# A graph network's edge search: the second half of each list one list later, and the first layer's weights prepared behind the first list

## The chip, the cores and the metric

One Trainium2 chip, one of its cores. The metric is device time in microseconds of one execution; a kernel's time is the median of several executions.

## The reference, cut to what matters

The inputs are node features `x` (4096 x 512, float) and an adjacency `adj` (4096 x 4096 of zeros and ones, from a model in which the low nodes have many neighbours and the high ones few). Two attention layers over the graph follow each other, each with a residual and a layer norm:

```python
x = _layernorm(x + _L0_gnn_ref(x, adj, L0_gnn_W, L0_gnn_a), axis=-1)
x = _layernorm(x + _L1_gnn_ref(x, adj, L1_gnn_W1, L1_gnn_a1, L1_gnn_Wo, L1_gnn_ao, ...), axis=-1)
```

Each attention is of this form (here the first, 8 heads of 64):

```python
h = jnp.einsum('nf,kfp->knp', node_matrix, W)
f1 = jnp.einsum('knp,kp->kn', h, a_src)
f2 = jnp.einsum('knp,kp->kn', h, a_dst)
e = jax.nn.leaky_relu(f2[:, :, None] + f1[:, None, :], negative_slope=ALPHA)
e = jnp.where(adjacency_matrix[None, :, :] > 0, e, NEG_INF)
att = jax.nn.softmax(e, axis=-1)
out = jnp.einsum('knm,kmp->knp', att, h)
```

The second layer has an 8-head attention, a one-head attention of width 512 and two dense layers (512 to 1024 to 512).

## The kernel before, in words

The kernel treats the adjacency as sparse. It has two parts, one after the other. First `find_edges` turns the dense adjacency into lists of neighbours (which column, for which row); then three attention passes (`heads_layer` twice, and a last one with the dense layers) gather rows of a table of projected features by these lists, weigh and add them. A dense path (`dense_path`) stands behind a branch that is taken only if a list overflows.

**Lists.** The 4096 rows are 32 tiles of 128 rows. Tile 0, whose rows have many neighbours, is cut by columns into four lists (0 to 256, 1024, 2304 and 4096); every other tile is one list, 35 lists in all. This text counts them 0 to 34: lists 0 to 3 are tile 0, list v above that is tile v - 3.

**First half of a list: the search.** ACT turns the loaded adjacency `raw` into signs `sg` (L848, one call for a whole tile, 128 x 4096). PE builds `key`, 1024 columns at a time, by two matmuls for each 512 columns (L877: the signs; L878: a place number for each column), into two PSUM buffers. DVE finds the eight largest keys of each segment of columns (`cand`, L884; in tile 0 three times with a `match_replace`, L887, between), and then, from the candidates, the k largest in order: `lst`, k/8 rounds of L899 and L901, each dependent on the one before. `over` (L896) is taken ahead of the first round. ACT makes column numbers `qs` and a count `balance` from `lst` (L906, L909); POOL makes `degs` and `counts` (L911 to L928).

**Second half of a list: the places.** PE sums the counts over the rows before (`prs`, L931), ACT makes each row's first and last place and two rows of signs `sides` (L932 to L943), POOL adds them to `s1` (L944) and prepares `rhs` and `rest` (L952 to L955). PE then multiplies these out into `pl` (L960, the "own" matmul with `own_b`, then pairs of L967 and L969), in one piece for most lists, in three or four pieces for lists 0 to 3; `pl` has one PSUM buffer. ACT copies `nl` and, for tile 0, `kk` out of it (L971, L984). DVE picks the column (`sel`: L986 one instruction for each group of 128 edges in tile 0, L977, L980 and L981 in the other lists), and POOL writes `idx` (L992 to L994).

**Beside it.** At the end of each tile's last list the loop calls `beside(t)`: it loads 128 rows of `x`, turns them (`pt`, L683, and `xt`, L686), projects them with layer 0's weights (`ph`, L697, eight matmuls a tile) and writes table rows (`hrow`, L710 and L711). For t = 8 and t = 16 it also calls `load_projection` for the next two weights. `load_projection` loads `sw` (L654 or L659) and `sab` (L663), POOL multiplies them (`sprod`, L667) and DVE reduces (`sw_t`, L672 or L677). After the loop `project_mean` projects the mean of all rows and writes one last table row.

**What sets the order.** This stage has no hand-written order. A scheduler takes the instructions in the order in which the program text traces them, as their priority, follows a model of when each can start, and writes one fixed queue for every engine. DMAs of this stage are issued on SP. The attention passes behind it do have an order written by hand. The first gather (L1084, POOL) belongs to tile 31, the last list, and needs that list's `idx`, the table with its last row, and a gather buffer cleared by ACT (L1297).

Of the kernel before, what the change touches and what calls it, by code (L numbers as in the profile page):

```python
# [10 lines left out]
F32 = mybir.dt.float32  # L11
BF16 = mybir.dt.bfloat16
# [3 lines left out]
AF = mybir.ActivationFunctionType  # L16
OP = mybir.AluOpType
AX = mybir.AxisListType
# [3 lines left out]
P = 128  # L22
N = 4096
# [20 lines left out]
FAR = -1e30  # L44
# [514 lines left out]
def sparse_path(  # L559
# [23 lines left out]
    nc = tc.nc  # L583
# [6 lines left out]
    most = max(p.blocks for p in pts)  # L590
    longest = max(p.n for p in pts)
    kmax = max(p.k for p in pts)
# [8 lines left out]
    ident_b = const.tile([P, P], BF16, name="s_identb")  # L601
# [10 lines left out]
    half = const.tile([P, 2], F32, name="half")  # L612
# [10 lines left out]
    s1 = const.tile([P, blocks_ * P], BF16, name="s1")  # L623
# [14 lines left out]
    st0 = Stage2("t0", 8, 64, dest_first=False)  # L638
# [212 lines left out]
    def find_edges(big, sb, ps, pk, constants, sg, beside):  # L851
# [8 lines left out]
        starts = big.tile([P, nv], F32, name="starts")  # L860
        ends = big.tile([P, nv], F32, name="ends")
        degsum = big.tile([P, 1], F32, name="degsum")

        for v, p in enumerate(pts):
            t, k, c0, nch = p.t, p.k, p.first, p.n
            if t > 0:
# [28 lines left out]
            last = cand.rearrange("p (s e) -> p s e", e=r8)[:, skip:, r8 - 1]  # L895
# [9 lines left out]
            qs = sb.tile([P, kmax + 1], F32, name="qs")[:, : k + 1]  # L905
# [4 lines left out]
            deg = degs[:, v : v + 1]  # L910
# [16 lines left out]
            else:  # L927
                nc.gpsimd.tensor_copy(counts[:, v : v + 1], deg)  # L928
            deg = counts[:, v : v + 1]
            prs = ps.tile([P, 1], F32, name="prs", tag="small")  # L930
            nc.tensor.matmul(prs, before, deg, start=True, stop=True)  # L931
            nc.scalar.activation(qs[:, k:], prs, AF.Identity, bias=ends_at[:, v : v + 1], scale=-1.0)  # L932

            lim = sb.tile([P, 1], F32, name="lim")
            nc.gpsimd.tensor_sub(lim, deg, mids[:, v : v + 1])
            first = starts[:, v : v + 1]
            nc.scalar.activation(first, prs, AF.Identity, bias=mids[:, v : v + 1], scale=-1.0)
            nc.scalar.activation(ends[:, v : v + 1], prs, AF.Identity, bias=lim)
            wide = p.blocks * P
            here = s1[:, p.at * P : p.at * P + wide]  # L940
            sides = sb.tile([P, 2, most * P], BF16, name="sides")[:, :, :wide]
            nc.scalar.activation(sides[:, 0], iota_e[:, :wide], AF.Sign, bias=first)
            nc.scalar.activation(sides[:, 1], iota_e[:, :wide], AF.Sign, bias=ends[:, v : v + 1], scale=-1.0)  # L943
            nc.gpsimd.tensor_add(here, sides[:, 0], sides[:, 1])  # L944


            rhs = sb.tile([P, 2 * (kmax + 2)], BF16, name="rhs")[:, : 2 * (k + 2)].rearrange("p (h w) -> p h w", h=2)
            rest = sb.tile([P, 2 * (kmax + 1)], BF16, name="rest")[:, : 2 * (k + 1)].rearrange("p (h w) -> p h w", h=2)
            q2 = sb.tile([P, 2 * (kmax + 1)], F32, name="q2")[:, : 2 * (k + 1)].rearrange("p (h w) -> p h w", h=2)
            shape = [P, 2, k + 1]  # L950
            for h in range(2):
                nc.scalar.activation(rhs[:, h, : k + 1], qs, AF.Copy, scale=half[:, h : h + 1])  # L952
            nc.gpsimd.tensor_mul(q2, qs[:, None, :].to_broadcast(shape), half[:, :, None].to_broadcast(shape))
            nc.gpsimd.tensor_sub(rest, q2, rhs[:, :, : k + 1])
            nc.gpsimd.tensor_copy(rhs[:, :, k + 1], row1)  # L955
            per = 512 // (k + 2)
            for lo in range(0, nch, per):
                m = min(per, nch - lo)
                pl = ps.tile([P, m, k + 2], F32, name="pl")
                nc.tensor.matmul(  # L960
                    pl, ident_b, own_b[:, None, kmax - k :].to_broadcast([P, m, k + 2]), start=True, stop=False
                )
                last = None
                for block, groups, chunks in blocks_in(p, lo, m):
                    for of, w in ((rhs, k + 2), (rest, k + 1)):
                        if last:
                            nc.tensor.matmul(*last, start=False, stop=False)  # L967
                        last = pl[:, chunks, :w], s1[:, ts(p.at + block, P)], of[:, groups, :w]
                nc.tensor.matmul(*last, start=False, stop=True)  # L969
                cs = slice(c0 + lo, c0 + lo + m)  # L970
                nc.scalar.copy(nl[:, cs], pl[:, :, k + 1])  # L971
                nc.gpsimd.tensor_scalar(hole[:, cs, 0], nl[:, cs], -0.5, FAR, op0=OP.is_lt, op1=OP.mult)
                src = sb.tile([P, longest], F32, name="src")[:, :m]
                sel = sb.tile([P, 512], F32, name="sel")[:, : m * k].rearrange("p (m k) -> p m k", k=k)
                if k < 100:
                    shape = [P, m, k]
                    nc.vector.tensor_tensor(  # L977
                        sel, iota_k[:, lo : lo + m, :k], pl[:, :, k : k + 1].to_broadcast(shape), op=OP.is_equal
                    )
                    nc.vector.tensor_tensor(sel, sel, pl[:, :, :k], op=OP.mult)  # L980
                    nc.vector.tensor_reduce(src, sel, AX.X, OP.add)  # L981
                else:
                    kk = sb.tile([P, longest], F32, name="kk")[:, :m]
                    nc.scalar.copy(kk, pl[:, :, k])  # L984
                    for c in range(m):
                        nc.vector.scalar_tensor_tensor(  # L986
                            sel[:, c], iota_k[:, lo + c, :k], kk[:, c : c + 1], pl[:, c, :k],
                            op0=OP.is_equal, op1=OP.mult, accum_out=src[:, c : c + 1],
                        )

                past = sb.tile([P, longest], F32, name="past")[:, :m]
                nc.gpsimd.tensor_scalar(past, nl[:, cs], -0.5, 2.0 * N, op0=OP.is_lt, op1=OP.mult)  # L992
                nc.gpsimd.tensor_add(past, past, src)
                nc.gpsimd.tensor_copy(idx[:, cs], past)  # L994
            if p.last:
                beside(t)


        nc.vector.tensor_tensor(over[:, 1], degs, by_parts("room_k", lambda p: p.k - 0.5), op=OP.is_gt)
        groups = by_parts("room_n", lambda p: p.chunks[0] * P)  # L1000
# [369 lines left out]
    with ExitStack() as pools:  # L1370
        big = pools.enter_context(tc.tile_pool(name="eb", bufs=1))
        sb = pools.enter_context(tc.tile_pool(name="es", bufs=2))
        sg0 = signs_of(sb, 0, 8)
        constants = edge_constants(big)
        load_projection(big, st0, w0, a0)
        ps = pools.enter_context(tc.tile_pool(name="ep", bufs=1, space=PSUM))
        pp = pools.enter_context(tc.tile_pool(name="eq", bufs=2, space=PSUM))
        pk = pools.enter_context(tc.tile_pool(name="ek", bufs=2, space=PSUM))

        def beside(t):  # L1380
            xr = sb.tile([P, F], F32, name="xr")
# [16 lines left out]
    sb = ctx.enter_context(tc.tile_pool(name="ls", bufs=2, reuse_waits="tile"))  # L1398
# [30 lines left out]
    with tc.tile_pool(name="tb", bufs=1, side="right", reuse_waits="tile") as big, \  # L1429
# [95 lines left out]
        for last, block in zip(blocks, blocks[1:]):  # L1525
            chunks = sum(u.n for u in units if u.t in block)
# [91 lines left out]
```

## Time and profile before

| what | us |
|---|---|
| median of 3 executions | 2126.52 (2125.99 to 2130.2) |
| the profiled execution, its own time | 2338.45 |
| its span in the trace | 2336.3 |
| granted TensorE clock in it | 0.879 |
| first gather (L1084) starts, from the span's start | 502.94 |

The profiled execution is longer than the others; durations below are all of that one. The page gives PE 76%, DVE 57%, ACT 28% and POOL 49% busy over the whole span. In the page's rows, a group is `line engine op out<-in xcount | busy, mean ns | idle before, releaser`. In a timeline, a row is start, duration, engine, line, operation, and in brackets how long the engine sat idle before it and what ended that. The costliest groups of the edge search are these (page, part 5):

```profile
L884 DVE MAX8 cand<-key 128x8 f32<-128x353 f32 (+55 forms) x467 | 196.3, 446 | 79.5 <-PE key L878 78.9
L877 PE MATMUL key<-sg,s_identb 128*128 128x512 bf16 (+1 forms) x258 | 111.9, 435 | 14.5 <-DVE cand L884 9.0
L848 ACT ACTIVATE sg<-raw 128x4096 bf16<-128x4096 int32 (+1 forms) x39 | 117.0, 2999 | 9.4 <-PE key L877 5.0
```

### The profile page before, as it was taken

What the parts mean: (1) busy time and instruction counts of PE and PEld (TensorE: products, weight loads), DVE (VectorE), ACT (ScalarE), POOL (GpSimd) and SP (SyncE); (2) the same over time, 40 slices, a digit from 0 to 9 for tenths busy, and PEclk for the clock granted to TensorE, in tenths of its full rate; (3) what the DMA queues carried; (4) which work ended last, traced back from release to release, by engine and by line L of the source; (5) the groups of instructions that cost most, each with busy time, mean ns of one, the idle gap of its engine ahead of it and who ended that gap; (6) DMA issues with size and microseconds to landing.
All of it is one profiled execution on the core that took longest, in us unless ns stands there. A gap on an engine that the chain in (4) does not pass through costs nothing.

```text
span 2336.3 us, 29301 instructions
## 1 busy us (share of the span) xinstructions
PE 1771.7 (76%) x8987; PEld 1040.1 (45%) x8987; DVE 1331.3 (57%) x3933; ACT 660.7 (28%) x2316; POOL 1151.6 (49%) x1658
## 2 busy tenths in 40 slices
PE   4777776645677787764667687666999898998997
PEld 3655442213444564432444465434545443444444
DVE  5887777745676797744555676653343424334322
ACT  3446776650222222111222232211111011111221
POOL 5424444456555666536556666536355634445300
PEclk9889997866878899876788899887999998999999
DMA  6434565536666667526555556436254624335301
GB/s 214 132 129 158 219 241 220 213 83 179 181 175 182 197 208 224 166 76 163 154 140 145 159 158 186 133 110 191 85 156 126 172 82 148 101 109 150 90 19 51
DMA packets 132589, 351.94 MB, mean 151 GB/s; under 512 B 41922, under 2 KB 42954, under 8 KB 128454
## 3 DMA queue, kind: packets, MB, share of 16 engines
q0 software_dynamic: 74160, 206.25, 32.5%
q1 hardware_dynamic: 58262, 143.72, 17.3%
q8 instruction: 74, 1.21, 0.2%
q14 instruction: 93, 0.76, 0.1%
HBM read 347.31 MB, written 42.24 MB: 167 GB/s over the span
## 4 chain that ended last, share of the span: by engine, by line
PE 46%; DVE 16%; issue 13%; ACT 7%; another core or an unknown queue 7%; POOL 6%; DMA 4%; SPq 0%; DVEq 0%; POOLq 0%; ACTq 0%
PE acc L1220 15%; PE ph L697 11%; PE p L1495 10%; PE p L1507 5%; DVE g L1208 3%; POOL g L1084 2%; DMA xr<-sx_d 2%; DVE cand L884 2%; DMA g<-table_t,idx 2%; PE pt L683 1%; POOL s L944 1%; DVE cand L901 1%; DVE lst L899 1%; ACT sides L943 1%
## 5 line engine op out<-in xcount | busy, mean ns | idle before, releaser
L1084 POOL DMA_INDIRECT g<-table_t,idx x927 | 937.2, 1011 | 769.4 <-PE acc L1220 336.4
L1220 PE MATMUL acc<-g,sm 128*64 128x260 f32 (+2 forms) x4068 | 587.9, 414 | 175.3 <-DVE g L1208 91.7
L697 PE MATMUL ph<-sw_t,xt 128*128 128x264 f32 (+1 forms) x1536 | 436.4, 437 | 146.5 <-ACT xt L686 80.6
L1220 PEld LDWEIGHTS acc<-g,sm 128*64 128x64 f32 x4068 | 332.9, 146 | 395.1 <-issue 123.9
L697 PEld LDWEIGHTS ph<-sw_t,xt 128*128 128x128 f32 x1536 | 323.0, 217 | 229.2 <-ACT xt L686 97.9
L1208 DVE TENSOR_TENSOR g<-g,wp 128x2048 f32<-128x2048 f32 (+4 forms) x134 | 349.3, 2607 | 37.9 <-ACT wp L1163 18.7
L884 DVE MAX8 cand<-key 128x8 f32<-128x353 f32 (+55 forms) x467 | 196.3, 446 | 79.5 <-PE key L878 78.9
L1495 PE MATMUL p<-sht,sl1w 128*128 128x512 f32 (+1 forms) x576 | 229.0, 553 | 5.5 <-issue 4.9
L1507 PE MATMUL p<-sl2w,shid 128*128 128x512 f32 x512 | 227.2, 598 | 0.0
L686 ACT ACTIVATE xt<-pt 128x128 f32<-128x128 f32 x384 | 101.5, 279 | 292.9 <-PE pt L683 122.1
L710 ACT COPY hrow<-ph 128x260 f32<-128x260 f32 (+2 forms) x194 | 71.9, 374 | 320.2 <-PE ph L697 186.9
L1495 PEld LDWEIGHTS p<-sht,sl1w 128*128 128x128 f32 x576 | 107.7, 191 | 116.9 <-issue 112.0
L1507 PEld LDWEIGHTS p<-sl2w,shid 128*128 128x128 f32 x512 | 95.4, 190 | 120.4 <-issue 119.6
L1257 DVE SCALAR_TENSOR_TENSOR o<-ex,o 128x512 f32<-128x512 f32 x64 | 44.5, 695 | 179.2 <-ACT ex L1256 150.0
L877 PE MATMUL key<-sg,s_identb 128*128 128x512 bf16 (+1 forms) x258 | 111.9, 435 | 14.5 <-DVE cand L884 9.0
L848 ACT ACTIVATE sg<-raw 128x4096 bf16<-128x4096 int32 (+1 forms) x39 | 117.0, 2999 | 9.4 <-PE key L877 5.0
L1498 ACT ACTIVATE shid<-p,sl1b 128x512 f32<-128x512 f32 (+1 forms) x72 | 46.0, 640 | 244.5 <-PE p L1495 221.0
L878 PE MATMUL key<-frac,places 128*128 128x512 bf16 (+1 forms) x258 | 112.0, 435 | 2.6 <-POOL places L784 2.6
L1195 DVE TENSOR_SCALAR sm<-iota_n,nl,w 128x64 f32<-128x64 f32 x339 | 83.5, 328 | 31.9 <-ACT w L1166 31.9
L1155 DVE TENSOR_TENSOR z<-s,g 128x16 f32<-128x16 f32 (+9 forms) x294 | 44.7, 174 | 82.9 <-DMA g<-table_t,idx 81.2
L686 ACT ACTIVATION_READ_ACCUMULATOR xt<-pt 128x1 f32 x384 | 79.9, 208 | 0.0
L1228 DVE RECIPROCAL rd<-acc 128x8 f32<-128x8 f32 x64 | 13.1, 205 | 114.4 <-PE acc L1220 73.3
(184 smaller groups left out, 1812.8 us busy)
## 6 DMA issues: line engine op xcount, KB each, us to landing
raw<-in_adj_dram SPq DMA_DIRECT2D x31, 2048.0 KB
table_t<-hrow SPq DMA_DIRECT2D x64, 260.0 KB
xr<-in_x_dram SPq DMA_DIRECT2D x64, 256.0 KB
g<-table_t,idx POOLq DMA_INDIRECT x927
table_t<-hrow SPq DMA_DIRECT2D x32, 257.0 KB
sx_d<-o SPq DMA_DIRECT2D x32, 256.0 KB
xr<-sx_d SPq DMA_DIRECT2D x32, 256.0 KB
out_dram<-xr SPq DMA_DIRECT2D x32, 256.0 KB
```

The lines of the kernel that those rows point to most:

```text
L686: nc.scalar.activation(xt[:, c, :], pt[:, c, :], AF.Copy, accum_out=st.xparts[:, c, t : t + 1])
L697: nc.tensor.matmul(ph[:n], columns(c), st.w[:, c, j], start=(c == 0), stop=(c == FC - 1))
L848: nc.scalar.activation(sg[:, ts(i, w)], raw[:, ts(i, w)], AF.Sign)
L877: nc.tensor.matmul(out_, ident_b, sg[:, j:e], start=True, stop=False)
L878: nc.tensor.matmul(out_, places[:, w], frac[:, j - w * KW : e - w * KW], start=False, stop=True)
L884: nc.vector.max(out=cand[:, at : at + 8], in_=part)
L1084: nc.gpsimd.indirect_dma_start(out=u.g[:, k, : self.st.row], out_offset=None, in_=self.st.table[:, :], in_offset=bass.IndirectOffsetOnAxis ...
L1195: nc.vector.tensor_scalar(sm[:, at + i], of_g, node[k], u.w[:, k], op0=OP.is_equal, op1=OP.mult)
L1208: nc.vector.tensor_mul(body, body, wp[:, :, :, None].to_broadcast(body.shape))
L1220: nc.tensor.matmul(out_[g * HN : (g + 1) * HN], sm[:, slot], rows(k), start=start, stop=stop)
L1495: nc.tensor.matmul(p1, l1w[:, c, ts(k, P)], hts[b][:, c, :n], start=(c == 0), stop=(c == FC - 1))
L1507: nc.tensor.matmul(p2, hids[b][:, k, ts(j, P)], l2w[:, k, :], start=(k == 0), stop=(k == HC - 1))
```

## The change

Two edits. The second half of a list, from `prs` to `idx`, becomes a function `place` that is put on a list; it is called one list later, after the next list's search has been traced (and before that list's `beside`), the last one after the loop. And `load_projection` for layer 0 isn't called ahead of `find_edges` any more: the loop calls `beside(-1)` after the first list, which calls it. What is computed stays the same. The diff, cut where lines are only indented:

```diff
+        places_of = []
         for v, p in enumerate(pts):
             t, k, c0, nch = p.t, p.k, p.first, p.n
...
             deg = counts[:, v : v + 1]
-            prs = ps.tile([P, 1], F32, name="prs", tag="small")
-            nc.tensor.matmul(prs, before, deg, start=True, stop=True)
-            nc.scalar.activation(qs[:, k:], prs, AF.Identity, bias=ends_at[:, v : v + 1], scale=-1.0)
...
+            def place(v=v, p=p, k=k, c0=c0, nch=nch, qs=qs, deg=deg):
+                prs = ps.tile([P, 1], F32, name="prs", tag="small")
+                nc.tensor.matmul(prs, before, deg, start=True, stop=True)
+                nc.scalar.activation(qs[:, k:], prs, AF.Identity, bias=ends_at[:, v : v + 1], scale=-1.0)
...
+                    nc.gpsimd.tensor_copy(idx[:, cs], past)
+
+
+            places_of.append(place)
+            if len(places_of) > 1:
+                places_of.pop(0)()
+            if v == 0:
+                beside(-1)
             if p.last:
                 beside(t)
+        places_of.pop(0)()
...
         sg0 = signs_of(sb, 0, 8)
         constants = edge_constants(big)
-        load_projection(big, st0, w0, a0)
         ps = pools.enter_context(tc.tile_pool(name="ep", bufs=1, space=PSUM))
...
         def beside(t):
+            if t < 0:
+
+                load_projection(big, st0, w0, a0)
+                return
             xr = sb.tile([P, F], F32, name="xr")
```

More of the change, by code (lines that the diff above doesn't have):

```diff
@@ L929, in find_edges @@
             deg = counts[:, v : v + 1]
-            prs = ps.tile([P, 1], F32, name="prs", tag="small")
-            nc.tensor.matmul(prs, before, deg, start=True, stop=True)
-            nc.scalar.activation(qs[:, k:], prs, AF.Identity, bias=ends_at[:, v : v + 1], scale=-1.0)
[L934 to L944, printed above, removed]
@@ L947, in find_edges @@
[L947 to L978, printed above, removed]
-                    )
[L980 to L988, printed above, removed]
-                        )
[L991 to L994, printed above, removed]
@@ new lines, in place @@
+            def place(v=v, p=p, k=k, c0=c0, nch=nch, qs=qs, deg=deg):
+                prs = ps.tile([P, 1], F32, name="prs", tag="small")
+                nc.tensor.matmul(prs, before, deg, start=True, stop=True)
+                nc.scalar.activation(qs[:, k:], prs, AF.Identity, bias=ends_at[:, v : v + 1], scale=-1.0)
+                lim = sb.tile([P, 1], F32, name="lim")
+                nc.gpsimd.tensor_sub(lim, deg, mids[:, v : v + 1])
+                first = starts[:, v : v + 1]
+                nc.scalar.activation(first, prs, AF.Identity, bias=mids[:, v : v + 1], scale=-1.0)
+                nc.scalar.activation(ends[:, v : v + 1], prs, AF.Identity, bias=lim)
+                wide = p.blocks * P
+                here = s1[:, p.at * P : p.at * P + wide]
+                sides = sb.tile([P, 2, most * P], BF16, name="sides")[:, :, :wide]
+                nc.scalar.activation(sides[:, 0], iota_e[:, :wide], AF.Sign, bias=first)
+                nc.scalar.activation(sides[:, 1], iota_e[:, :wide], AF.Sign, bias=ends[:, v : v + 1], scale=-1.0)
+                nc.gpsimd.tensor_add(here, sides[:, 0], sides[:, 1])
+                rhs = sb.tile([P, 2 * (kmax + 2)], BF16, name="rhs")[:, : 2 * (k + 2)].rearrange("p (h w) -> p h w", h=2)
+                rest = sb.tile([P, 2 * (kmax + 1)], BF16, name="rest")[:, : 2 * (k + 1)].rearrange("p (h w) -> p h w", h=2)
+                q2 = sb.tile([P, 2 * (kmax + 1)], F32, name="q2")[:, : 2 * (k + 1)].rearrange("p (h w) -> p h w", h=2)
+                shape = [P, 2, k + 1]
+                for h in range(2):
+                    nc.scalar.activation(rhs[:, h, : k + 1], qs, AF.Copy, scale=half[:, h : h + 1])
+                nc.gpsimd.tensor_mul(q2, qs[:, None, :].to_broadcast(shape), half[:, :, None].to_broadcast(shape))
+                nc.gpsimd.tensor_sub(rest, q2, rhs[:, :, : k + 1])
+                nc.gpsimd.tensor_copy(rhs[:, :, k + 1], row1)
+                per = 512 // (k + 2)
+                for lo in range(0, nch, per):
+                    m = min(per, nch - lo)
+                    pl = ps.tile([P, m, k + 2], F32, name="pl")
+                    nc.tensor.matmul(
+                        pl, ident_b, own_b[:, None, kmax - k :].to_broadcast([P, m, k + 2]), start=True, stop=False
+                    )
+                    last = None
+                    for block, groups, chunks in blocks_in(p, lo, m):
+                        for of, w in ((rhs, k + 2), (rest, k + 1)):
+                            if last:
+                                nc.tensor.matmul(*last, start=False, stop=False)
+                            last = pl[:, chunks, :w], s1[:, ts(p.at + block, P)], of[:, groups, :w]
+                    nc.tensor.matmul(*last, start=False, stop=True)
+                    cs = slice(c0 + lo, c0 + lo + m)
+                    nc.scalar.copy(nl[:, cs], pl[:, :, k + 1])
+                    nc.gpsimd.tensor_scalar(hole[:, cs, 0], nl[:, cs], -0.5, FAR, op0=OP.is_lt, op1=OP.mult)
+                    src = sb.tile([P, longest], F32, name="src")[:, :m]
+                    sel = sb.tile([P, 512], F32, name="sel")[:, : m * k].rearrange("p (m k) -> p m k", k=k)
+                    if k < 100:
+                        shape = [P, m, k]
+                        nc.vector.tensor_tensor(
+                            sel, iota_k[:, lo : lo + m, :k], pl[:, :, k : k + 1].to_broadcast(shape), op=OP.is_equal
+                        )
+                        nc.vector.tensor_tensor(sel, sel, pl[:, :, :k], op=OP.mult)
+                        nc.vector.tensor_reduce(src, sel, AX.X, OP.add)
+                    else:
+                        kk = sb.tile([P, longest], F32, name="kk")[:, :m]
+                        nc.scalar.copy(kk, pl[:, :, k])
+                        for c in range(m):
+                            nc.vector.scalar_tensor_tensor(
+                                sel[:, c], iota_k[:, lo + c, :k], kk[:, c : c + 1], pl[:, c, :k],
+                                op0=OP.is_equal, op1=OP.mult, accum_out=src[:, c : c + 1],
+                            )
+                    past = sb.tile([P, longest], F32, name="past")[:, :m]
+                    nc.gpsimd.tensor_scalar(past, nl[:, cs], -0.5, 2.0 * N, op0=OP.is_lt, op1=OP.mult)
+                    nc.gpsimd.tensor_add(past, past, src)
+                    nc.gpsimd.tensor_copy(idx[:, cs], past)
```

## The prediction

> **What bounds the kernel now.** I read, in this order: the busy slices of the page, the waits of VectorE (DVE) up to 500 us, the stages by windows, then single stretches of the timeline. The change touches only the stage that searches the adjacency's edges, which ends when the first gather (L1084) is issued at 502.94 us; what follows can only shift with it.
>
> The windows cut this stage at the starts of `prs` (L931) of lists 0, 1, 2 and 3, then later. Columns: PE, PEld, DVE, ACT, POOL busy, granted clock, DMA share, GB/s.
>
> ```profile
> 0.00:43.60 43.60, 15.85 (x55) 10.50 (x55) 24.24 (x113) 14.94 (x41) 26.04 (x110) 1.00 0.76 246
> 43.60:81.70 38.10, 28.89 (x137) 21.83 (x137) 30.43 (x142) 15.45 (x80) 16.73 (x28) 0.84 0.56 165
> 81.70:124.30 42.60, 34.84 (x152) 26.23 (x152) 34.27 (x149) 18.59 (x79) 17.03 (x32) 0.82 0.37 127
> 124.30:165.40 41.10, 32.03 (x165) 23.21 (x165) 38.09 (x192) 19.27 (x83) 8.71 (x30) 0.92 0.31 105
> ...
> 203.60:361.40 157.80, 120.51 (x641) 69.29 (x639) 119.56 (x407) 115.27 (x306) 66.08 (x237) 0.96 0.60 221
> 361.40:490.00 128.60, 83.92 (x350) 30.26 (x350) 91.59 (x280) 79.81 (x163) 54.41 (x217) 0.76 0.48 179
> ```
>
> Up to 165 us (tile 0's four lists) DVE carries the stage: where it is idle, something named made it wait, and the waits view says what:
>
> ```profile
> DVE cand L884 <- PE key L878: 78.9, 60, 5.7
> DVE sel L986 <- ACT kk L984: 17.3, 10, 3.5
> DVE sw_t L672 <- POOL sprod L667: 11.6, 14, 4.6
> ```
>
> (us in total, times, longest.) The second and third lines are tile 0; 73.2 of the first line's 78.9 us lie behind 187 us, in lists 4 to 34. There no engine is full (DVE 119.56 of 157.80 us) and the lists follow each other as a loop through all engines. One turn, on PE and then DVE:
>
> ```profile
> 364.91 0.20 PE L967 MATMUL pl<-rhs,s 128*128 128x52 bf16 x1 [2.14 <-POOL s L944]
> ...
> 365.32 0.38 PE L877 MATMUL key<-sg,s_identb 128*128 128x512 bf16 x1
> ...
> 366.38 0.23 DVE L884 MAX8 cand<-key 128x8 f32<-128x66 f32 x1 [2.28 <-PE key L878]
> ```
>
> The reader is to see: `pl` waits for `s`, the next keys stand behind `pl` in PE's queue, and DVE waits for those keys; from them come the next list's last `lst`, then ACT, POOL, `prs`, ACT, `s` again. `prs` recurs every 10.1 us from list 20 to 27 (361.4 to 432.0) and every 8.6 us from 28 to 33 (442.5 to 485.7).
>
> The stage's end:
>
> ```profile
> 491.52 2.80 PE L697 MATMUL ph<-sw_t,mean 128*1 128x264 f32 x6 [0.72 <-DVE mean L739]
> 494.25 0.59 PE L931 MATMUL prs<-counts,before 128*128 128x1 f32 x2
> ...
> 497.55 0.60 PE L697 MATMUL ph<-sw_t,mean 128*1 128x264 f32 x2
> 498.09 0.20 PE L967 MATMUL pl<-rhs,s 128*128 128x52 bf16 x1
> ...
> 502.94 1.31 POOL L1084 DMA_INDIRECT g<-table_t,idx  x1 [2.78 <-DMA xr<-in_x_dram]
> ```
>
> The projection of the mean stands twice before work of the last list, and the gather starts 2.78 us after `idx` is ready.
>
> **What the Trainium skill says.** "PSUM — Partial Sum Buffer", section "Engine vs sequencer instructions": the queues of ACT, DVE and GpSimd are strict FIFO and matmuls start and complete in program order. The trace agrees (DVE idles 2.28 us at L884 with other work behind it), so the order of instructions decides here. "VectorE: DVE Perf Modes", section "The DRAIN you can't avoid": the next operation does not start until the pipe is empty, though one that is not held starts earlier. The trace shows the second: independent rows overlap (MAX8 at 147.93 for 0.42, the next at 148.27), dependent ones do not (110.07 for 0.40, the next at 110.50). "DMA: Bandwidth & Descriptors", section "Anatomy of one DMA": about 2 us fixed per transfer, mostly the write's receipt; the mean row's DMA, issued at 498.90, and the gather at 502.94 fit that, with some 2 us of issue more.
>
> **The change part by part.** No instruction is added or removed: both programs have the same numbers on every engine. A scheduler lists them, so I compared the two orders list by list (list v counts 0 to 34; 0 to 3 are tile 0). The second half already ran about one list late: before `sel` of list v stand 14 to 18 `cand` of later lists, before and after alike, from list 14 to 29. So the edit is a new tie-break, not a new pipeline; its sizes are small.
>
> 1. Weights of layer 0. The DMAs and POOL's eight `sprod` keep their places, so the last L672 still starts at 29.17. Before, twelve short operations of list 0 stood behind it until `over` at 31.43; now they stand between the eight, where DVE waited for POOL (1.55, 1.85, 0.53... us), and `over` follows at once, about 29.85: **-1.6**.
> 2. `sel` of lists 0 to 3 (L986, 51 pieces, 18.4 us idle: 5.1, 4.3, 2.5, 6.2 by list). In lists 0 to 2 the pieces move back by 1 to 7 places at the first and 14, 30 and 23 at the last, one at a time between searches instead of by fours. I worked list 0: the second `kk` still comes at 55.6, because 3.4 us of `ph` and `pt` stand before its `own` on PE, so only about 1.4 of 5.1 us goes. I take 1.8, 1.5 and 1.5 for the others (in list 3 `sel` keeps its place, but nine more `cand` of list 4 are left to cover its chain): **-6.2**, with ends 0 and -14.
> 3. Filling. Two rounds of `lst` with two `cand` between cost 1.07 us (147.93 to 149.01), a bare round of a slightly shorter list 0.94: an independent operation between dependent ones costs some 0.1 us less than alone. 38 pieces so placed, half of them beside others already: **-2**, ends 0 and -5.
> 4. Weights of layer 1. Their eight L672 wait for `sprod`, 1.23 us each, from the arrival of `sab` at 67.8; that DMA stands on SP behind the table row of tile 3 (62.40). Reaching them 3 us earlier is worth nothing unless that row is earlier too; `pt` of tile 3 is now listed before the second `pl` of list 0, some 2 us. I give back half: **+1.5**, ends 0 and +3.
> 5. Projections as filler. At `prs` of list 3 PE has passed 208 instead of 220 of them, by list 19 it is level: twelve matmuls, 4.1 us at 0.44 for `ph` and 0.15 for `pt`, go into lists 4 to 18, where PE is 76% busy. Half on the path: **+2**, ends 0 and +4.
> 6. The loop. It is open where part of the list after next's first keys is issued before `pl` (18 or more key matmuls of later lists). Before: lists 6, 10, 13, 17 and 28 to 32; after: 6, 22, 27, 28, 29. Four fewer, at up to 1.45 us (10.1 less 8.6; part of that is the smaller `sides` from list 26 on). Against it, `prs` mostly stands behind a full third window (12 keys, before 8 to 10 in many lists), and L977 behind the last `lst`, 0.25 us. **+2**, ends -8 and +12.
> 7. The end. All of the mean's projection and its row's DMA now lie at list 20 and 21, behind `key`s. `prs` no longer stands behind `ph` (0.4), nor `pl` (0.45), DVE has two operations fewer before the last `lst` (0.3), and the gather doesn't wait for the row but for ACT's first clearing L1297 (501.8 less 0.35): about 1.2. **-2.3**, ends -1 and -3.
>
> Sum -1.6 -6.2 -2 +1.5 +2 +2 -2.3 = -6.6 us of the profiled execution's 2338.45 us (span 2336.3 and 2.15 around it). The timed median, 2126.52, is 0.909 of that; I take the gain in the same proportion, -6.0: **2120.5 us**.
>
> **Rivals.** (a) The loop shortens as well: the later place of L977 and of `prs` saves 0.3 us in each of 28 lists, -8.4 instead of +2: -17 in all, 2111. For it: DVE waits 2 us behind `prs` in several turns. Against: the loop, not DVE, holds the period where `pl` stands at 16. (b) No change: tile 0's gain in lists 0 and 1 is lost in the wait for `sab`, and the rest pays for filler: about -2, 2125. For it: sprod's pace is fixed; L672 is 11.6 us of the waits. (c) **Slower**: PE's queue closes the loop. `pl` of list v ahead of the keys of list v+2 costs 1.45 us a turn; if eight lists pay it (+11.6), the filler costs its full 4 and `sel` gains only 3, the sum is -1.6 -3 +1.5 +4 +11.6 -2.3 = +10, or 2135.5. It decides from about six more lists that pay, against 8.6 us of gains without point 6. For it: four fewer open lists, and 30 to 32 are now all at 16. (d) That the change does nothing in lists 4 to 34 because the scheduler had done it already: that is my case, with point 6 near nothing.
>
> **How the numbers follow.** The forecast 0.45 (own range 2114 to 2127), (a) 0.15, (b) 0.20, (c) 0.20. A median can be told from no change from about 0.2%, 4.3 us. Below 2122.3 lie seven tenths of the forecast, all of (a) and little of (b): faster 0.50; same 0.29; slower 0.21. Range 2109 to 2134, which cuts the far halves of (a) and (c).
>
> **What would show it.** Right: `over` of list 0 near 29.9; L986's waits near 12 instead of 18.4 us; `prs` of list 4 some 7 us before 175.6; no `ph<-sw_t,mean` after 480; the gather less than 1.8 us after the last `idx`. Point 4 is wrong if `sab` of layer 1 lands at 67.8 again. I am wrong if `prs` recurs every 10 us from list 30 on, or if the 7 us are gone by list 20.

## The result, and the profile after

The changed kernel takes 2118.48 us (median of 10 executions, 2112.59 to 2127.98), the kernel before 2127.68 us (10 executions, 2125.99 to 2133.16): a ratio of 0.9957, with a 95% interval of 0.9945 to 0.9969, or 9.2 us less. A second comparison on another chip gave 0.9958 (0.9941 to 0.9976).

The first profiled execution of before lasted 2338.45 us and that of the change 2112.59 us, so their spans can't be compared. The stage of the edge search can. Two more profiles of before (e5 and e12 below) and one more of the change (e10) put its first gather at nearly the same place, whatever the whole execution took. The stage is cut here at `over` of list 4 (where tile 0's search is done), at `over` of list 34 and at the first gather:

| stretch, us | before: first, e5, e12 | after: first, e10 | means differ by |
|---|---|---|---|
| start to `over` of list 4 | 161.79, 162.13, 160.21 | 154.03, 153.57 | -7.6 |
| from there to `over` of list 34 | 328.19, 326.33, 326.32 | 323.46, 326.76 | -1.8 |
| from there to the first gather | 12.96, 12.96, 12.96 | 11.91, 11.92 | -1.0 |
| first gather | 502.94, 501.42, 499.49 | 489.40, 492.25 | -10.5 |

The windows of the third profile of before (e12), cut at these places, show what DVE did in each. Columns: window and length, PE, PEld, DVE, ACT and POOL busy (with instructions), granted clock, DMA share, GB/s.

```profile
8.00:160.21 152.21, 104.57 (x489) 76.79 (x489) 122.42 (x577) 62.78 (x272) 59.87 (x170) 0.92 0.48 155
160.21:486.53 326.32, 235.50 (x1209) 120.08 (x1208) 242.64 (x812) 221.39 (x552) 142.06 (x522) 0.88 0.53 195
486.53:499.49 12.96, 8.48 (x52) 3.27 (x52) 6.05 (x30) 7.25 (x15) 4.63 (x20) 0.76 0.15 50
```

The same windows of the changed kernel:

```profile
8.00:154.03 146.03, 104.05 (x482) 76.17 (x481) 119.06 (x579) 59.33 (x261) 59.94 (x170) 0.89 0.48 156
154.03:477.49 323.46, 236.39 (x1231) 122.11 (x1231) 241.65 (x812) 224.45 (x565) 142.94 (x522) 0.90 0.55 202
477.49:489.40 11.91, 3.54 (x34) 2.33 (x35) 5.24 (x28) 6.45 (x13) 4.60 (x20) 0.54 0.01 3
```

In the first window DVE does as many instructions (577 and 579) in 3.4 us less busy time; the rest of the gain there is idle time. In the last one PE has 18 matmuls fewer; 16 of them are the mean's projection, which in the change runs from 349.8 to 358.5 us.

The waits of DVE in the changed kernel up to 487 us (us in total, times, longest), beside the three lines of before shown in the prediction:

```profile
DVE cand L885 <- PE key L879: 74.4, 55, 5.7
DVE sel L988 <- ACT kk L986: 16.3, 9, 5.3
DVE sw_t L672 <- POOL sprod L667: 9.4, 15, 3.3
```

The wait of `sel` for `kk`, in which the forecast saw its largest gain, is almost what it was over all four lists (17.3 before). Up to `over` of list 4 it is 2.6 us shorter (11.2 and 8.6 in the means of the profiles); the pieces of list 3, which come later, wait longer. Where the busy time went is in DVE's timeline. Before, the pieces of `sel` stand by fours; this is the second group of list 0:

```profile
55.68 0.32 DVE L986 SCALAR_TENSOR_TENSOR sel<-iota_k,kk,pl 128x104 f32<-128x104 f32 x1 [2.08 <-ACT kk L984]
55.93 0.08 DVE L986 DVE_READ_ACCUMULATOR sel<-iota_k,kk,pl 128x1 f32 x1
55.93 0.32 DVE L986 SCALAR_TENSOR_TENSOR sel<-iota_k,kk,pl 128x104 f32<-128x104 f32 x1
```

After, the same group with searches of list 1 between its pieces:

```profile
54.27 0.32 DVE L988 SCALAR_TENSOR_TENSOR sel<-iota_k,kk,pl 128x104 f32<-128x104 f32 x1 [2.43 <-ACT kk L986]
54.52 0.08 DVE L988 DVE_READ_ACCUMULATOR sel<-iota_k,kk,pl 128x1 f32 x1
54.52 0.26 DVE L885 MAX8 cand<-left 128x8 f32<-128x101 f32 x1
54.70 0.07 DVE L888 MATCH_VALUE_LOAD left<-cand,key 128x8 f32 x1
54.76 0.21 DVE L888 MATCH_REPLACE8 left<-cand,key 128x58 f32<-128x58 f32 x1
54.88 0.31 DVE L988 SCALAR_TENSOR_TENSOR sel<-iota_k,kk,pl 128x104 f32<-128x104 f32 x1
```

The wait ahead of the group is no shorter (2.43 against 2.08 us). From the MAX8 on every row begins before the one in front of it has ended: 54.52 plus 0.26 is 54.78, and the next two begin at 54.70 and 54.76. Rows overlap before the change, too, and many of the search's rows here are narrower than those behind the group before, so this one group shows how the pieces stand and not what that is worth.

The first window as a whole shows it. The durations of all its rows add up to 147.5 to 148.0 us before and to 147.0 and 147.1 after; with overlaps counted once, DVE is busy 122.4 to 122.5 and 118.9 to 119.1 us. The overlap of the 38 pieces of `sel` with the rows next to them grew from 6.0 to 8.6 us, 0.07 us a piece. The overlap of the search's rows with each other stayed (16.5 to 16.9 before, 16.8 after), though 29 fewer of them stand next to each other: the pieces went to places where search rows had not overlapped.

That is 2.6 of the 3.4 us. The rest, 0.9 us, is one instruction of a projection, first before (e12), then after:

```profile
86.79 1.21 DVE L723 TENSOR_TENSOR s<-ss_t,half 128x128 f32<-128x128 f32 x1
91.15 0.27 DVE L723 TENSOR_TENSOR s<-ss_t,half 128x128 f32<-128x128 f32 x1
```

It takes 1.21 us in the three profiles of before and 0.27 to 0.29 in the eleven of all other kernels. In the three, a POOL instruction of 2.36 us (L944) is running when it begins, and it ends 0.15 us after that one; in the change POOL runs nothing then. That POOL holds it up was not tested.

The end of the stage:

```profile
481.32 0.59 PE L933 MATMUL prs<-counts,before 128*128 128x1 f32 x2 [3.06 <-POOL counts L927]
...
484.56 0.23 PE L969 MATMUL pl<-rhs,s 128*128 128x52 bf16 x1 [0.67 <-POOL s L946]
...
489.40 1.42 POOL L1094 DMA_INDIRECT g<-table_t,idx  x1 [2.49 <-PE pss L1126]
```

`prs` and `pl` of the last list wait for their own operands only, with no `ph` ahead; the gather starts 2.49 us after `idx`, where it was 2.78. What it waits for fits the clearing of its buffer by ACT: the first clearing ends at 488.51 us, 0.89 us ahead of the gather, and it is 0.89 us in all eleven profiles of kernels other than before. In the three of before it is 1.18 us.

### The profile page after: what moved, and what is told of

Same layout as the page of the kernel before. It is cut to its first block, busy times and chain, and to the rows that moved or that the text cites. A ratio compares the mean times of both kernels' runs of the same rounds, so it can differ in the third digit from the quotient of the medians.

```text
span 2110.3 us, 29302 instructions
## 1 busy us (share of the span) xinstructions
PE 1707.7 (81%) x8987; PEld 999.2 (47%) x8987; DVE 1323.1 (63%) x3933; ACT 663.4 (31%) x2316; POOL 1155.6 (55%) x1658
## 3 DMA queue, kind: packets, MB, share of 16 engines
q8 instruction: 74, 1.21, 0.2%
## 4 chain that ended last, share of the span: by engine, by line
PE 34%; DVE 19%; issue 15%; POOL 13%; DMA 12%; ACT 6%; SPq 1%; POOLq 0%; DVEq 0%; ACTq 0%
PE acc L1230 11%; PE p L1508 10%; DMA g<-table_t,idx 10%; POOL g L1094 9%; PE ph L697 5%; DVE g L1218 5%; PE p L1520 4%; DVE cand L885 2%; DMA xr<-sx_d 1%; DVE cand L902 1%; POOL s L946 1%; DVE lst L900 1%; ACT sides L945 1%; POOL sprod L667 1%; DVE sm L1197 1%
## 5 line engine op out<-in xcount | busy, mean ns | idle before, releaser
L1230 PE MATMUL acc<-g,sm 128*64 128x260 f32 (+2 forms) x4068 | 580.8, 415 | 175.1 <-DVE g L1218 141.8
L1230 PEld LDWEIGHTS acc<-g,sm 128*64 128x64 f32 x4068 | 328.3, 147 | 391.8 <-DVE g L1218 156.8
L697 PE MATMUL ph<-sw_t,xt 128*128 128x264 f32 (+1 forms) x1536 | 394.0, 404 | 51.5 <-ACT xt L686 51.3
L697 PEld LDWEIGHTS ph<-sw_t,xt 128*128 128x128 f32 x1536 | 291.9, 197 | 120.0 <-ACT xt L686 72.3
L1520 PEld LDWEIGHTS p<-sl2w,shid 128*128 128x128 f32 x512 | 95.2, 190 | 119.9 <-issue 119.4
L878 PE MATMUL key<-sg,s_identb 128*128 128x512 bf16 (+1 forms) x258 | 109.7, 426 | 20.6 <-DVE cand L885 11.1
L1205 DVE TENSOR_SCALAR sm<-iota_n,nl,w 128x64 f32<-128x64 f32 x339 | 83.8, 327 | 30.8 <-ACT w L1176 30.8
L1173 ACT ACTIVATE wp<-z 128x32 f32<-128x32 f32 (+4 forms) x134 | 27.5, 205 | 207.0 <-DVE g L1218 206.5
L1525 DVE TENSOR_TENSOR xr<-p,xr 128x512 f32<-128x512 f32 x32 | 22.0, 688 | 94.1 <-PE p L1520 93.6
```

What stands on the lines that cost most here:

```text
L697: nc.tensor.matmul(ph[:n], columns(c), st.w[:, c, j], start=(c == 0), stop=(c == FC - 1))
L878: nc.tensor.matmul(out_, ident_b, sg[:, j:e], start=True, stop=False)
L1205: nc.vector.tensor_scalar(sm[:, at + i], of_g, node[k], u.w[:, k], op0=OP.is_equal, op1=OP.mult)
L1230: nc.tensor.matmul(out_[g * HN : (g + 1) * HN], sm[:, slot], rows(k), start=start, stop=stop)
L1520: nc.tensor.matmul(p2, hids[b][:, k, ts(j, P)], l2w[:, k, :], start=(k == 0), stop=(k == HC - 1))
```

## The experiments

Times against runs of before on the same chip; the gather is from the profile of the same kernel.

| run | us | before | ratio, 95% interval | first gather |
|---|---|---|---|---|
| e1 weights only | 2132.99 | 2128.23 | 1.0022, 1.0014 to 1.003 | 505.23 |
| e2 second half only | 2119.88 | 2128.23 | 0.996, 0.9942 to 0.9977 | 491.10 |
| e3 late in lists 0 to 2 only | 2125.52 | 2128.23 | 0.9991, 0.9981 to 1.0002 | 498.38 |
| e4 late from list 3 on only | 2124.12 | 2128.23 | 0.9981, 0.997 to 0.9992 | 496.75 |
| e6 two lists late | 2295.28 | 2323.81 | 0.989, 0.985 to 0.993 | 473.44 |
| e7 `pl` late alone | 2310.99 | 2323.81 | 0.9955, 0.9934 to 0.9977 | 495.29 |
| e8 as e6, mean earlier | 2102.77 | 2132.0 | 0.9857, 0.9839 to 0.9875 | 475.20 |
| e9 as e8, three lists late | 2105.65 | 2132.0 | 0.9875, 0.9859 to 0.9892 | 477.83 |
| e10 the change again | 2311.18 | 2320.81 | 0.9958, 0.9941 to 0.9976 | 492.25 |
| e11 as e7 again | 2317.92 | 2320.81 | 0.9989, 0.9964 to 1.0014 | 493.63 |

e5 and e12 are the kernel before, for their profiles (2309.07 and 2314.1 us).

**e1 to e4: the change in parts.** e1 is the kernel before with the weights moved as in the change; its second halves stay where they were:

```diff
+            if v == 0:
+                beside(-1)
             if p.last:
                 beside(t)
...
-        load_projection(big, st0, w0, a0)
```

e2 leaves the weights ahead of all lists (`load_projection` back before `find_edges`, no `beside(-1)`). e3 and e4 are the change with

```diff
-            if len(places_of) > 1:
+            while len(places_of) > (1 if v < 3 else 0):
```

and, for e4, `v >= 3` in place of `v < 3`. e3 has no call left behind the loop.

> Only the first layer's weights stand behind list 0; every second half is called at once, as before. Theory (my sum, point 1): over of list 0 comes 1.6 us earlier and all that follows is shifted by it, -1 to -2 us of the time. Rival A (the shift seen between the two profiles, over of list 0 28.42 instead of 31.43, is the weights' alone and passes through): -3 us. Rival B (the gain is swallowed by the wait for layer 1's weights): 0, prs of list 3 where it was. Rival C (the scheduler's order of the lists 4 to 34 comes from where list 0 begins, so this edit carries most of the change): -6 us or more.

> Only the second half of a list's way is put behind the next list's first half; layer 0's weights are prepared ahead of all lists, as before. Theory: it carries what the weights do not: -6 to -8 us of the change's -9.2, with over of list 0 near 31.4 again. Rival B (the two parts only work together: an earlier list 0 gives nothing if its second half stands at once behind it, and the other way round): -3 us or less. Rival C (the weights carry it): 0.

> Weights as in the change; the second half is one list late for lists 0 to 2 only, and is called at once from list 3 on. Theory of my forecast (tile 0 holds the gain, lists 4 to 34 are unaffected or lose a little by it): -7 us or more, up to the whole -9.2. Rival (a) of the forecast (the loop of lists 4 to 34 shortens by itself): -3 to -5 us, with a lead of 7 us at prs of list 4 that does not grow to list 34.

> Weights as in the change; the second half is called at once for lists 0 to 2, and is one list late from list 3 on. Theory of my forecast: -1.6 us from the weights and 0 or +2 from lists 4 to 34, so between -2 and 0. Rival (a): the loop's own shortening, -5 to -7 us, with a lead at prs of list 4 of 2 to 3 us that grows to 8 or more at list 34.

What the profiles show of tile 0, by whether the second half is late in lists 0 to 2 (us; busy and waits of DVE from 8 us to `over` of list 4):

| kernel | weights late | second half late | `over` list 0 | `over` list 4 | DVE busy | `sel` waits for `kk` |
|---|---|---|---|---|---|---|
| before (3) | no | no | 31.43, 31.29, 30.79 | 161.79, 162.13, 160.21 | 122.49, 122.45, 122.42 | 11.1, 11.8, 10.6 |
| e1 | yes | no | 28.30 | 160.64 | 121.46 | 14.5 |
| e4 | yes | no | 28.84 | 162.40 | 121.45 | 15.0 |
| e2 | no | yes | 31.05 | 159.02 | 119.37 | 11.7 |
| e3 | yes | yes | 27.93 | 152.52 | 118.86 | 7.9 |
| after (2) | yes | yes | 28.42, 28.83 | 154.03, 153.57 | 119.06, 118.93 | 9.2, 8.0 |

The weights alone bring list 0 forward by 2.3 to 2.9 us, and it is all lost by list 4. In lists 0 to 2 DVE comes to the first `sel` 1.6 to 3.8 us earlier than before, but `kk` only 0.4 to 2.6 us earlier, and the wait between them grows from about 11 to 14.5 and 15.0. Of the 1.0 us less busy time in e1 and e4, 0.9 is L723. Later second halves alone gain 2.4 us there (161.38, the mean of before, less 159.02), with 3.1 us less busy time. Together they gain 7.4 to 8.9. So no theory on e1 was right; with its later turns (below) it is slower by more than its interval. The weights' part pays only together with the later second halves; that the searches of the next list then fill the time until `kk` fits the shorter waits (7.9 to 9.2). The theory of e2 was right in the sum, not in the place: most of e2's gain comes after tile 0.

For the lists behind, the sum of the turns (from `prs` to the next `prs`, us, by list), and the number of key matmuls of list v + 2 that stand ahead of `pl` of list v for v = 26 to 29, counted in the order of PE's instructions:

| kernel | 4-9 | 10-19 | 20-25 | 26-29 | 30-33 | sum | keys ahead, 26 to 29 |
|---|---|---|---|---|---|---|---|
| before, first | 85.1 | 100.8 | 59.8 | 38.7 | 34.3 | 318.7 | 0, 1, 4, 3 |
| e5 and e12 | 84.1 | 98.8 | 60.6 | 38.6 | 34.3 | 316.5 | the same |
| e1 | 85.2 | 101.6 | 60.6 | 38.3 | 34.3 | 319.9 | 0, 1, 4, 3 |
| e3 | 86.4 | 100.9 | 58.8 | 38.3 | 34.1 | 318.4 | 0, 1, 4, 3 |
| after, first | 82.5 | 98.8 | 58.9 | 34.5 | 36.0 | 310.7 | 0, 12, 12, 2 |
| e10 | 84.0 | 99.1 | 60.5 | 34.4 | 36.3 | 314.3 | 0, 12, 12, 2 |
| e2 | 83.3 | 97.4 | 58.1 | 34.8 | 35.2 | 308.8 | 0, 0, 12, 12 |
| e4 | 83.4 | 98.7 | 61.2 | 30.8 | 36.8 | 310.8 | 12, 12, 12, 2 |
| e7 | 83.5 | 99.0 | 60.7 | 37.5 | 36.1 | 316.8 | 0, 3, 3, 1 |
| e11 | 81.0 | 100.1 | 60.1 | 38.7 | 36.0 | 315.8 | 0, 3, 3, 1 |

The clearest gain stands in lists 26 to 29. A list there with 12 keys ahead took 8.1 to 8.6 us as the first of its run and 6.4 to 7.3 behind the first; before, list 26 took 10.8 us with no key ahead, list 27 10.5 with one and list 28 8.2 with four. e4 seems to gain twice as much with three such lists, but its list 25, counted in the column before, took 12.8 us instead of 9.1. Over lists 24 to 29 the four profiles with 12 keys ahead somewhere take 54.1 to 54.9 us and the seven others 57.6 to 59.4: some 4 us, for two lists as for three.

Lists 30 to 32 had 4, 3 and 4 keys ahead before and have none in the change, and lists 30 to 33 lose 1.8 us. e7 and e11 have 3, 1 and 3 there and lose as much, so the bare number of keys doesn't explain it. In lists 4 to 25 the two profiles of the change (240.2 and 243.6 in sum) are further apart than their mean is from the mean of before (244.2). The other versions say more: lists 4 to 23 take 219.5 to 223.1 us in the six profiles of kernels with `pl` one list late from list 3 on (the change, e2, e4, e7, e11), and 223.8 to 227.4 in the five of the others (before, e1, e3). So a part of the gain is probably spread over these lists, and the keys ahead don't explain that part.

The rival of e3 and e4 was nearer than the theory, with smaller numbers: e3 leads by 5.4 us at `prs` of list 4 (170.02, before 175.39 in the mean) and by 4.1 at list 34, and its time is 2.7 us less, with an interval that includes no change; e4 is 2.4 us behind at list 4, leads by 3.9 at list 34, and takes 4.1 us less.

**e5, e12: before again.**

> The kernel before, once more, for a trace from an execution of the usual length (the first profiled one took 2338.45 us). If the stages of the edge search were as long there as usual, prs of lists 0, 4 and 34 come within 1 us of 43.61, 175.56 and 494.25 and the first gather near 502.9; if that execution was already disturbed in this stage, they come 2 to 4 us earlier, and part of the lead that the change shows in the traces (13.5 us at the first gather against 9.2 us of the time) was never there.

> The kernel before, for a trace from the same chip as e10 and e11: turns of lists 4 to 33 between 316 and 319 us in sum, first gather between 501 and 503 us.

The gather came at 501.42 us in e5, between its two readings, and at 499.49 in e12, earlier than expected there. The first profile had it 1.5 to 3.5 us later, by 2.1 us in a single turn (list 14 took 11.6 us there, 9.5 in e5). The lead of 13.5 us between the two first profiles is 10.5 between the means, and 7.2 between e12 and e10, which ran on one chip.

**e6: two lists late.** `qs` gets a third buffer, and a second half waits for two searches:

```diff
-            qs = sb.tile([P, kmax + 1], F32, name="qs")[:, : k + 1]
+            qs = sb.tile([P, kmax + 1], F32, name="qs", bufs=3)[:, : k + 1]
...
-            if len(places_of) > 1:
+            if len(places_of) > 2:
...
-        places_of.pop(0)()
+        while places_of:
+            places_of.pop(0)()
```

> The change with the second half two lists late instead of one (qs gets a third buffer). On PE eight matmuls of the keys of list v+2 then stand ahead of pl of list v in every list, where in the change it is none in most. Theory L (the turn of lists 4 to 34 is closed through PE's queue: lst, counts, prs, sides, pl, the key of the list after next behind it, its cand ahead of the next lst on DVE): every turn opens, prs recurs every 9 us or less instead of 10.1 us in lists 10 to 27, prs of list 34 comes 15 to 30 us before the 481 us of the change, and the time is some 2095 us. Rival (DVE's and PE's own work sets the turn and the order between them no longer matters): within 3 us of the change, 2116 to 2121. Rival (the third buffer's depth costs at the end, where two second halves stand behind the last list): slower than the change by up to 8 us.

The turns of lists 4 to 33 came to 296.3 us, the gather to 473.44, and the time to 0.989 of before. That is theory L in its mechanism, with smaller numbers: `prs` recurs every 9.1 us in lists 10 to 27, not 9 or less, and the ratio stands for some 2104 us where 2095 was expected (an estimate from the 2127.68 us of the first comparison). The last rival is right about the end, which takes 15.76 us from `over` of list 34 instead of 11.9, and wrong about the sum. This is a turn of the changed kernel, in its timeline:

```profile
360.89 0.38 PE L933 MATMUL prs<-counts,before 128*128 128x1 f32 x2 [0.94 <-POOL counts L927]
...
364.38 0.20 PE L969 MATMUL pl<-rhs,s 128*128 128x52 bf16 x1 [2.14 <-POOL s L946]
...
364.79 0.38 PE L878 MATMUL key<-sg,s_identb 128*128 128x512 bf16 x1
...
365.86 0.24 DVE L885 MAX8 cand<-key 128x8 f32<-128x69 f32 x1 [2.28 <-PE key L879]
...
366.01 0.15 DVE L897 TENSOR_REDUCE over<-cand 128x1 f32<-128x11 f32 x1
366.08 0.24 DVE L900 MAX8 lst<-cand 128x8 f32<-128x88 f32 x1
```

`pl` waits 2.14 us for `s` and holds the keys behind it; DVE waits 2.28 us for the first of them, with `over` and `lst` of the next list behind that `cand`. It is the turn of before, row by row. With two lists:

```profile
364.67 0.38 PE L933 MATMUL prs<-counts,before 128*128 128x1 f32 x2 [2.25 <-POOL counts L927]
364.91 0.38 PE L878 MATMUL key<-sg,s_identb 128*128 128x512 bf16 x1
...
369.25 0.19 PE L969 MATMUL pl<-rhs,s 128*128 128x52 bf16 x1
...
373.40 0.38 PE L933 MATMUL prs<-counts,before 128*128 128x1 f32 x2 [1.55 <-POOL counts L927]
```

The keys now follow `prs`, and `pl` comes when `s` has long been there. The turn is 8.7 us, and what is late next is `prs`: it stands ahead of those keys and waits for `counts`. The waits of PE from `over` of list 4 to `over` of list 34 say it for all lists. Before (e12):

```profile
PE prs L931 <- POOL counts L926: 33.2, 29, 2.1
PE pl L967 <- POOL s L944: 29.3, 29, 2.2
```

Two lists late (e6):

```profile
PE prs L933 <- POOL counts L927: 49.3, 23, 4.4
```

No wait for `s` is left among its groups, and 16 us of it came back in front of `prs`. The rows agree with "PSUM — Partial Sum Buffer", section "Engine vs sequencer instructions", of the Trainium skill, by which matmuls start in program order: a `prs` or `pl` that waits holds every key listed behind it.

**e7, e11: `pl` late alone.** `prs`, `sides`, `s`, `rhs` and `rest` are called at once, and the rest of `place`, from `pl` on, one list later:

```diff
                 nc.gpsimd.tensor_copy(rhs[:, :, k + 1], row1)
+                return rhs, rest
+
+            def expand(v=v, p=p, k=k, c0=c0, nch=nch, of2=None):
+                rhs, rest = of2
                 per = 512 // (k + 2)
...
-            places_of.append(place)
+            places_of.append(partial(expand, of2=place()))
```

> As the change, but prs, sides, s, rhs and rest of a list are called at once, and only pl with all behind it (nl, sel, idx) one list later. If it is the later place of pl and of sel that shortens the turns, the sum of the turns of lists 4 to 33 is near the 310 us of the change (before 319) and the time about 2119. If it is the later place of prs and of the signs on ACT, the sum stays near 319 and the time at 2124 to 2128.

> The change once more, beside e11 and on the same chip. If the order in the queues sets the turns, the sum of the turns of lists 4 to 33 repeats within 2 us (310.7 in its first profile), the first gather comes 10 to 13 us before that of the kernel before, and the ratio is 0.9945 to 0.9969 again.

> The kernel of e7 once more, beside the change. In e7 the turns did not shorten (316.8 us), but the time came out like the change's, with an interval of 0.4% that holds both readings. If the turns tell the time, it is 3 to 6 us slower than e10 with turns near 317; if they do not, it is level with e10.

The turns stay those of before, 316.8 and 315.8 us. The time of e7 came out level with the change; beside the change on one chip, in e11, it is 6.7 us slower than e10 (2317.92 and 2311.18) and not told from before, though the ends of the two intervals still meet. So later `pl` and `sel` alone do not shorten the sum of the turns: the keys of list v + 2 got ahead of `pl` by twelve only where `prs` and the signs were late as well. For e10 the ratio repeated; the turns repeated to 3.6 us, not to the 2 expected, and its gather came 7.2 us before that of e12, not 10 to 13.

**e8, e9: the mean earlier, and three lists.** e8 calls `project_mean` ahead of the two last second halves; e9 has in addition a fourth `qs` and `> 3`. This is e8 against e6:

```diff
+        beside(NT)
         while places_of:
             places_of.pop(0)()
...
+            if t == NT:
+                project_mean(sb, pp, st0)
+                return
...
-        project_mean(sb, pp, st0)
```

> Two lists late as in e6, and the mean's projection called ahead of the two last second halves instead of behind them. In e6 the gather waited 4.30 us for the mean's row (2.78 or 2.49 in the others). Theory (that row ends the stage): the gather starts about 2.5 us after idx again and pl of the last list is not split by ph, so 2 to 4 us less than e6, 0.987 to 0.988 of before. Rival (the clearing of the gather's buffer by ACT ends the stage anyway): the same as e6, 0.989.

> As e8, with the second half three lists late (qs gets a fourth buffer). On PE all 16 key matmuls of list v+2 then stand ahead of pl of list v, instead of 8. Theory L: cand waits for key fall further (59.5 us in lists 4 to 34 of e6), the turns of lists 10 to 33 come from 216 us in sum to 200 to 208, and the time is 5 to 12 us below e8. Rival (with half of the keys ahead every turn was open already, and what is left is set by the key buffers that DVE frees): within 3 us of e8.

The gather's wait fell from 4.30 to 2.18 us. In e6 the clearing of its buffer stood on ACT behind the copy of the mean's row (469.48 us) and ended at 472.55; in e8 it ended at 474.31, and both gathers came 0.89 us later. So the clearing ends the stage, as the rival says, and in e6 the mean's projection had delayed it. But in e8 the projection stands ahead of `prs` of list 34, and the turn from list 33 to it took 12.6 us instead of 8.5. From `over` of list 34 to the gather it is 15.77 us against 15.76, so the edit gave nothing that the profile shows; the intervals of e6 and e8, on different chips, meet. e9 has all 16 keys ahead and isn't faster (turns 305.4, e8 301.1): PE waits for `counts` before `prs` for 50.9 us there. Its time is 2.9 us above e8, within the rival's 3. Theory L stops at `prs`.

e8 has the lowest ratio found, 0.9857 of before, against 0.9957 for the change; its interval meets those of e6 and e9.

## Why the prediction came out right, step by step

The time was forecast at 6.0 us less and is 9.2 less. In the profile the sum was -6.6 and the gather moved by -10.5. That tile 0 came out near its forecast is in part luck, because point 2 was 4 us too large and an instruction that stood in no term (L723) and a loss that didn't come (point 4) made up for most of it; behind tile 0 the forecast lost 1.7 us where 2.9 were gained.

- **Tile 0 (points 1 to 4): -8.3 forecast, -7.6 measured, but from other terms.** Point 1: `over` of list 0 came 2.5 us earlier, not 1.6, and e1 shows that this alone is lost by list 4. Point 2 is the term that was badly sized: -6.2 forecast, -2.1 measured (-3.3 in lists 0 to 2, which lie ahead of `over` of list 4). By list, the waits at L986 were 4.4, 4.0, 3.5 and 6.7 us (means of three profiles) and are 3.9, 0.2, 4.5 and 7.9 (of two). They left list 1 only; in lists 2 and 3 they grew, because DVE comes to `sel` sooner than `kk`. "L986's waits near 12" did not appear. Point 3, filling, held: -2 forecast, -2.6 measured as overlap of the pieces; busy time of e1 and e4 (121.5) against e2 and e3 (119.4, 118.9) puts about 2.3 on the later second halves. The 0.9 us of L723 stood in no term. Point 4 gave back 1.5 us for a `sab` that would be only half as early as the instructions that need it. The table row ahead of it on SP was earlier by all of it (issued at 58.86 instead of 62.40), and the first `sprod` came at 64.80 instead of 67.82, so there was nothing to give back: the waits at L672 and L677 stayed (14.1 and 13.8 us in the means).
- **Point 5, filler: +2 forecast, nothing seen.** Lists 4 to 19 took 182.9 to 185.9 us before and 181.3 and 183.2 after.
- **Point 6: +2 forecast; the turns got 4.7 us shorter** (means 317.2 and 312.5). Ahead of them 2.4 us are given back: the last `lst` of list 4, which stood ahead of the first `sel` of list 3, now stands behind it and its wait of 5.3 us, and `prs` of list 4 comes 16.4 us after its `over` instead of 14.0. So 1.8 is left between the `over`s. The mechanism was the right one, and the loss in lists 30 to 32 came as listed. What was mis-sized is the worth of an open list: each counted for at most 1.45 us, and list 28 with 4 keys ahead counted like list 28 with 12. Lists 27 and 28 brought 2.4 and 1.2 us (10.5 to 8.1, 8.2 to 7.0).
- **Point 7: -2.3 forecast, -1.0 measured.** The mean's projection left the end as foreseen, and the gather follows the clearing as foreseen. But it begins 0.89 us after the clearing has ended and not at once, so it gained 0.3 and not 1.2.
- **The scaling.** The gain was taken down by 0.909 because the profiled execution was long. The edge search wasn't: its gather repeats within 3.5 us in executions of 2309, 2314 and 2338 us. Unscaled, the forecast would have been 6.6.

Of the other signs, `prs` of list 4 came 5.2 us earlier in the means and not 7, the lead was still there at list 20 (6.8 us), and the gather came 2.5 us after `idx`, not within 1.8.

Of the rivals, (a) had the right sign for the turns at nearly twice the size (-8.4 for the loop, 4.7 less in the turns) and was wrong in the sum (-17 for the whole). (b) and (c) fall, though (c)'s mechanism fits what lists 30 to 33 pay; (c)'s sum also has no term for point 3. (d), no effect behind tile 0, can't be told from the two profiles of the change in lists 4 to 25, and the other versions speak against it.

What stays open: why the weights' earlier start costs e1 as much as 4.8 us in the whole (in its profile the gather is 2.3 to 5.7 us later than in the three of before), what shortens lists 4 to 23 where the second half is late, and what makes L723 long before.

## What to carry to other kernels

Where a loop runs through two in-order queues, find the instruction that waits at the head of one while work for the other stands behind it, and count how much of that work each turn lists ahead of it. If listing a second half one turn later opens few turns, try two before judging the idea: here it gave some two and a half times the gain (1.1% against 0.43%), until the next waiting instruction in the queue (`prs`) took over. An earlier start upstream of a wait can be lost in that wait when the other operand is not earlier by as much, as in e1; pair it with work that fills the wait. And before a difference in busy time is put down to the new order, look for single instructions whose duration changed: here one was a quarter of it.

## What the runs showed that was not expected

The same kernel took 2128 to 2132 us on two chips and 2321 to 2324 on two others. The edge search does not show it (first gather at 489.40 and 492.25 us in the two profiles of the change). The attention passes do: from 489 to 1000 us PE was busy 387.64 us at a granted clock of 0.90 in the one profile, and 355.95 us at 0.84 in the other; which of the two brings the other about isn't told by these runs.
